# Layer 1's vertical convolution: odd taps from shared row sums, and the difference of sums on GpSimd

## The chip, the cores and the metric

The kernel runs on one core of one Trainium2 chip. The metric is device time in microseconds (us) of one execution. A profile of one execution was taken for each kernel; its engines are called PE (TensorE matmuls), PEld (TensorE weight loads), DVE (VectorE), ACT (ScalarE), POOL (GpSimd) and SP (SyncE, which issues the DMAs).

## What is computed

The input `x` has shape (2, 128, 256, 256), in float32. There are two residual layers. Layer 0 is group norm followed by windowed attention; the change does not touch it. Layer 1 is group norm followed by a convolution block, cut here to what matters:

```python
x = x + _L0_conv_ref(_gn(x), ...)            # attention
x = x + _L1_conv_ref(_gn(x), w1, w3, w4)

def _L1_conv_ref(x, w1, w3, w4):
    t1 = conv(x, w1, padding=((2, 2), (0, 0)))       # 128 -> 128 channels, 5 taps down the rows
    t3 = conv(t1, w3, padding=((1, 1), (0, 0)), feature_group_count=c)   # 3 taps, per channel
    t2 = _unfold_w3_dil2(x)                          # columns -2, 0, +2
    t4 = einsum('nckhw,ckg->nghw', t2, w4)           # 8 group maps
    return t4[:, None] * t3.reshape(n, c // g, g, h, w)
```

The heavy part is `t1`: each output row is the sum of five 128 x 128 products with five neighbouring input rows.

## The kernel before

The 128 channels lie on the 128 partitions. Layer 1 (`convolutions_fast`) runs over 64 strips of 8 rows, 32 for each of the two batch items. Each engine carries out its instructions in the order in which the program text issues them. Engines meet only at semaphores.

Strip `k` of the main loop issues this, in this order:

1. `load_rows1(k+2)`: DMAs from SP.
2. `unfold(k)` (line 645): twelve small matmuls for `t4`, which ACT copies out (line 651).
3. `first_rows(k)`: ACT copies the two top rows of `t1` and one row of `p1` from the strip before (lines 682 and 683). In the first strip of a batch item matmuls make them.
4. `start_strip(k+1)`: ACT copies four normalised rows (604) and DVE normalises eight new ones (606). At a batch start the group norm's coefficients come first (lines 117 to 140).
5. `vertical(k, 2)`: the first four rows of `t1`, then ACT scales them by the first tap of `w3` (line 711).
6. `row_sums(k+1)`: ACT copies two old sums (631), DVE adds neighbouring rows into four new ones (632).
7. `depthwise(k, 2)`: two DVE instructions with two SBUF inputs each add the other two taps of `w3` (718).
8. `vertical(k, 4)` for the other four rows; `spread(k)` (729): four matmuls that copy `t4` to 128 channels.
9. `combine` (738) of two quarters on DVE, `depthwise(k, 4)` (718), `combine` of the other two.
10. `finish(k)`: POOL adds the residual rows in two instructions (746: three rows; 747: five rows), SP stores the strip.

The vertical taps use a fast algorithm that makes two output rows with three products of two-tap or three-tap polyphase filters. In `vertical(k, m)`, p1 (odd taps on odd rows), p0 (even taps on even rows) and p2 (sums of taps on sums of rows) are one PSUM tile of 512 columns each, that is two rows for a pair of pairs. p1 takes 2 matmuls, p0 takes 3, p2 takes 3; so 8 matmuls of 512 columns for four rows. ACT copies p1 to SBUF (696). DVE makes the even row as p0 + delayed p1 (698), `both` as p0 + p1 (700) and the odd row as p2 - `both` (706). The PSUM tiles of `taps` come from a pool of three buffers, so the fourth tile waits until the first has been read.

Float32 matmuls stand in the profile as two records each.

Of the kernel before, what the change touches and what calls it, by code (L numbers as in the profile page):

```python
# [9 lines left out]
F32 = mybir.dt.float32  # L10
I32 = mybir.dt.int32
AF = mybir.ActivationFunctionType
ALU = mybir.AluOpType
# [6 lines left out]
P = 128  # L20
W = 256
# [530 lines left out]
def convolutions_fast(tc, io, x1_d, norm, st_y, out):  # L552

    nc = tc.nc
    NB, _, H, _ = io["x"].shape
    NS = H // 8
    with ExitStack() as l1:
        cst = l1.enter_context(tc.tile_pool(name="f_l1c", bufs=1))
        rawp = l1.enter_context(tc.tile_pool(name="f_raw1", bufs=6))
        tp = l1.enter_context(tc.tile_pool(name="f_t1", bufs=2))  # L560
        wk = l1.enter_context(tc.tile_pool(name="f_wk1", bufs=2))
        ps_pj = l1.enter_context(tc.tile_pool(name="f_ps_pj1", bufs=1, space=PSUM))
        ps_a = l1.enter_context(tc.tile_pool(name="f_ps_a", bufs=3, space=PSUM))
        ps_b = l1.enter_context(tc.tile_pool(name="f_ps_b", bufs=1, space=PSUM))

        w1 = cst.tile([P, 5, P], F32, tag="w1", name="w1")
# [5 lines left out]
        sel = cst.tile([P, P], F32, tag="sel", name="sel")  # L572
        nc.sync.dma_start(sel, io["c_sel"])

        w1s = cst.tile([P, 2, P], F32, tag="w1s", name="w1s")
        nc.vector.tensor_add(w1s[:, 0], w1[:, 4], w1[:, 3])
        nc.vector.tensor_add(w1s[:, 1], w1[:, 2], w1[:, 1])
        xn = [cst.tile([P, 12, 260], F32, tag=f"xm{i}", name=f"xm{i}") for i in range(2)]
        for i in range(2):
            nc.gpsimd.memset(xn[i], 0.0)  # L580
# [29 lines left out]
                nc.gpsimd.memset(cur[:, 4 + n : 12, :], 0.0)  # L610

        norms = {}
        t1s, sms, p1s = {}, {}, {}

# [8 lines left out]
        def row_sums(k):  # L625
            s = k % NS
            xt = xn[k % 2]
            sms[k] = sm = tp.tile([P, 6, W], F32, tag="sm", name=f"sm_{k}")
            lo = 0 if s == 0 else 2
            if s > 0:  # L630
                nc.scalar.copy(sm[:, 0:2], sms[k - 1][:, 4:6])
            nc.vector.tensor_tensor(
                sm[:, lo:6], xt[:, 2 * lo : 12 : 2, 2 : 2 + W], xt[:, 2 * lo + 1 : 12 : 2, 2 : 2 + W],
                ALU.add,
            )

        ts = {}

# [17 lines left out]
        def taps(name, n, terms):  # L656
            pa = ps_a.tile([P, 512], F32, tag="a", name=f"a_{name}")
            for i, (w, rows) in enumerate(terms):
                nc.tensor.matmul(pa[:, : n * W], w, rows, start=i == 0, stop=i == len(terms) - 1)  # L659
            return pa[:, : n * W].rearrange("p (r w) -> p r w", w=W)  # L660

        def first_rows(k):

            s = k % NS
            xt = xn[k % 2]

            t1s[k] = t1 = tp.tile([P, 10, W], F32, tag="t1", name=f"t1_{k}")
            p1s[k] = p1 = tp.tile([P, 5, W], F32, tag="p1", name=f"p1_{k}")
            if s == 0:
                nc.gpsimd.memset(t1[:, 0:1, :], 0.0)  # L670
                top = taps(
                    f"{k}_first", 1,
                    [(w1[:, tap], xt[:, tap - 1 : tap, 2 : 2 + W]) for tap in (2, 3, 4)],
                )
                nc.scalar.copy(t1[:, 1:2, :], top)
                top = taps(
                    f"{k}_p1", 1,
                    [(w1[:, 3 - 2 * i], xt[:, 3 - 2 * i : 4 - 2 * i, 2 : 2 + W]) for i in range(2)],
                )
                nc.scalar.copy(p1[:, 0:1], top)  # L680
            else:
                nc.scalar.copy(t1[:, 0:2, :], t1s[k - 1][:, 8:10, :])
                nc.scalar.copy(p1[:, 0:1], p1s[k - 1][:, 4:5])
            if s + 1 == NS:
                nc.gpsimd.memset(t1[:, 9:10, :], 0.0)

        def vertical(k, m):

            s = k % NS
            xt, sm, t1, p1 = xn[k % 2], sms[k], t1s[k], p1s[k]  # L690

            def rows(j):
                return xt[:, j : j + 3 : 2, 2 : 2 + W]

            pa = taps(f"{k}_p1_{m}", 2, [(w1[:, 3 - 2 * i], rows(2 * m + 1 - 2 * i)) for i in range(2)])
            nc.scalar.copy(p1[:, m - 1 : m + 1], pa)
            pa = taps(f"{k}_p0_{m}", 2, [(w1[:, 4 - 2 * i], rows(2 * m - 2 * i)) for i in range(3)])
            nc.vector.tensor_tensor(t1[:, 2 * m - 2 : 2 * m + 1 : 2, :], pa, p1[:, m - 2 : m], ALU.add)
            both = wk.tile([P, 2, W], F32, tag="both", name=f"both_{k}_{m}")
            nc.vector.tensor_tensor(both, pa, p1[:, m - 1 : m + 1], ALU.add)  # L700
            pa = taps(
                f"{k}_p2_{m}", 2,
                [(w, sm[:, m - i : m - i + 2]) for i, w in enumerate((w1s[:, 0], w1s[:, 1], w1[:, 0]))],
            )
            n = 1 if m == 4 and s + 1 == NS else 2
            nc.vector.tensor_tensor(  # L706
                t1[:, 2 * m - 1 : 2 * m + 2 * n - 2 : 2, :], pa[:, 0:n], both[:, 0:n], ALU.subtract
            )
            t3 = ts[k][1]
            j = 2 * m - 4  # L710
            nc.scalar.activation(t3[:, j : j + 4], t1[:, j : j + 4, :], AF.Copy, scale=w3[:, 0:1])  # L711
# [39 lines left out]
        with tc.manual_schedule(engines=ORDERED):  # L751
            for k in range(2):
                load_rows1(*divmod(k, NS))
            start_strip(0)
            row_sums(0)
            for k in range(NB * NS):
                more = k + 1 < NB * NS
                if k + 2 < NB * NS:
                    load_rows1(*divmod(k + 2, NS))
                unfold(k)  # L760
                first_rows(k)
                if more:
                    start_strip(k + 1)

                vertical(k, 2)
                if more:
                    row_sums(k + 1)
                depthwise(k, 2)
                vertical(k, 4)
                banks = spread(k)  # L770
                combine(k, banks, (0, 1))
                depthwise(k, 4)
                combine(k, banks, (2, 3))
                finish(k)


def kernel_body(tc, io, out):
    nc = tc.nc
    NB, _, H, _ = io["x"].shape
    NS = H // 8  # L780
    with ExitStack() as ctx:
        glob = ctx.enter_context(tc.tile_pool(name="f_glob", bufs=1))
        dram = ctx.enter_context(tc.tile_pool(name="f_dram", bufs=1, space=DRAM))
        small = ctx.enter_context(tc.tile_pool(name="f_small", bufs=4))
        gavg = glob.tile([P, P], F32, tag="f_gavg", name="f_gavg")
        nc.sync.dma_start(gavg, io["c_gavg"])
        x1_d = [
            [dram.tile([P, 8, W], F32, tag=f"f_x1_{b}_{s}", name=f"f_x1_{b}_{s}") for s in range(NS)]
            for b in range(NB)
        ]  # L790
        norm = Norms(nc, glob, small, gavg, NS)
        tags = ("f_st0", "f_st1", "f_st2")
        st_x, st_y = {0: norm.new("f_st_x0", tags[0])}, {}
        ends = glob.tile([P, NB * NS], F32, tag="f_ends", name="f_ends")
        attention_fast(tc, io, x1_d, norm, st_x, st_y, tags, ends)
        good = in_range(tc, glob, ends)
        convolutions_fast(tc, io, x1_d, norm, st_y, out)
        count = nc.values_load(good, min_val=0, max_val=P)
    with tc.If(count < P):
        tile_halo_attention_then_conv(tc, io, out)  # L800
# [567 lines left out]
```

## Time and profile before

| | |
|---|---|
| median of 3 runs | 3296.84 us (3296.19 to 3297.35) |
| the profiled execution's own time | 3296.72 us |
| its span, first to last instruction | 3294.9 us |
| layer 1 | about 2118 us to the end, 64 strips |
| one strip in the steady state | 17.73 us, between equal instructions of neighbouring strips |

In the timeline of PE one strip is the sum of three stretches: `spread` 2780.28 to 2781.35, `unfold` to 2784.07, and the vertical taps to 2798.01, when the next `spread` starts. In each of the two batch items 31 strips follow one another at this pace; at the change of batch PE is idle for 7.60 us on DVE's statistics (line 117).

How to read the rows: in a timeline row the columns are start in us, length in us, engine, line, operation, output and inputs, shape, count, and in brackets the engine's idle time before it with what ended it. Lengths of consecutive DVE instructions overlap a little, because one starts before the one ahead of it has fully retired; so sums of work use distances from start to start.

### The profile page before, as it was taken

Reading aid. Unit: us, or ns where it says so; the run is one execution under the profiler, and the core shown is the slowest. Engines: PE = TensorE matmul, PEld = TensorE weight load, DVE = VectorE, ACT = ScalarE, POOL = GpSimd, SP = SyncE. Lnnn points to the kernel's source line nnn. Section 1 sums busy time; section 2 is a strip of 40 time slices with the busy share of each in tenths; the row PEclk is TensorE's granted clock in tenths of the full one; section 3 lists DMA queues with packets and bytes.
Section 4 is the critical chain, followed back from the end, with each engine's and each line's share of the span. In section 5 each row is a group of like instructions: output and inputs, shape, how many; then the busy total and the mean of one; then the engine's idle time right before and its main releaser. Section 6 shows DMA issues by size and latency. Waiting matters only on the chain.

```text
span 3294.9 us, 117110 instructions
## 1 busy us (share of the span) xinstructions
PE 3143.8 (95%) x52798; PEld 2244.1 (68%) x52798; DVE 2628.0 (80%) x4083; ACT 1499.9 (46%) x2543; POOL 935.7 (28%) x978
## 2 busy tenths in 40 slices
PE   0799999999999999999999999899999989999997
PEld 0688998998998889889988898633333333333333
DVE  8678888888888777777777777588888888888887
ACT  0455555555555555555555555333333323333332
POOL 2222222222222122222222222133433333433433
PEclk9999999999999999999999999999999999999999
DMA  9333323323323122122222222233333333333332
GB/s 400 117 105 128 118 96 127 116 97 127 115 100 122 62 86 86 67 83 85 72 83 81 76 83 70 76 103 125 105 128 119 111 102 128 110 120 128 104 126 86
DMA packets 115899, 360.34 MB, mean 109 GB/s; under 512 B 8000, under 2 KB 74304, under 8 KB 90816
## 3 DMA queue, kind: packets, MB, share of 16 engines
q1 hardware_dynamic: 115392, 352.76, 30.2%
q8 instruction: 419, 6.86, 0.8%
q14 instruction: 88, 0.72, 0.1%
HBM read 218.51 MB, written 134.22 MB: 107 GB/s over the span
## 4 chain that ended last, share of the span: by engine, by line
PE 95%; issue 2%; DVE 1%; POOL 1%; DMA 1%; ACT 0%; SPq 0%; POOLq 0%; DVEq 0%
PE a_p L659 27%; PE f_pv L399 14%; PE f_pq L324 8%; PE f_s L434 8%; PE f_o L459 8%; PE f_pk L324 7%; PE f_py L324 7%; PE g L645 5%; PE f_pa L378 4%; PE f_s L418 4%; PE b L729 2%; DMA f_sx<-in_x 0%; DVE t L718 0%; POOL f_xn L189 0%; DMA raw<-f_x 0%
## 5 line engine op out<-in xcount | busy, mean ns | idle before, releaser
L405 DVE COPY f_vt<-f_pv 64x512 f32<-64x512 f32 x512 | 354.5, 695 | 299.2 <-ACT f_vt L405 299.0
L659 PE MATMUL a_p<-xm,w 128*128 128x512 f32 (+1 forms) x1288 | 580.5, 596 | 0.0
L306 POOL COPY f_xq<-f_xn 128x256 f32<-128x256 f32 x512 | 309.1, 648 | 763.7 <-DVE f_xn L292 763.7
L399 PE MATMUL f_pv<-f_wqkvT,f_xn 128*128 128x128 f32 x4096 | 491.3, 278 | 0.0
L399 PEld LDWEIGHTS f_pv<-f_wqkvT,f_xn 128*128 128x128 f32 x4096 | 466.9, 192 | 8.6
L659 PEld LDWEIGHTS a_p<-xm,w 128*128 128x128 f32 x1288 | 237.9, 188 | 330.8 <-issue 330.5
L443 ACT ACTIVATE f_p<-f_s 128x512 f32<-128x512 f32 x512 | 264.4, 604 | 406.0 <-PE f_s L434 406.0
L359 ACT ACTIVATE f_q<-f_pq,f_head 128x512 f32<-128x512 f32 x512 | 310.4, 688 | 297.1 <-PE f_pq L324 297.0
L711 ACT ACTIVATE t<-t,w 128x1024 f32<-128x1024 f32 x128 | 147.3, 1150 | 619.1 <-DVE t L706 619.1
L718 DVE SCALAR_TENSOR_TENSOR t<-t,w,t 128x1024 f32<-128x1024 f32 x256 | 420.2, 1642 | 6.8 <-ACT t L711 1.7
L405 ACT COPY f_vt<-f_pv 64x512 f32<-64x512 f32 x512 | 298.0, 582 | 119.0 <-PE f_pv L399 118.2
L746 POOL TENSOR_TENSOR y<-y,raw 128x768 f32<-128x768 f32 x62 | 169.5, 2734 | 540.1 <-DVE y L738 493.0
L283 POOL COPY f_xn<-f_xn 128x1280 f32<-128x1280 f32 x62 | 86.7, 1398 | 780.7 <-PE f_pv L399 780.7
L747 POOL TENSOR_TENSOR y<-y,raw 128x1280 f32<-128x1280 f32 x64 | 246.4, 3850 | 164.3 <-DVE y L738 164.3
L434 PEld LDWEIGHTS f_s<-f_q,f_kt 64*64 64x64 f32 x16384 | 251.6, 135 | 49.6 <-issue 49.2
L324 PE MATMUL f_pq<-f_xn,f_wq_s 128*128 128x160 f32 (+1 forms) x1536 | 277.0, 327 | 0.9 <-issue 0.9
L434 PE MATMUL f_s<-f_q,f_kt 64*64 64x64 f32 x16384 | 269.2, 220 | 0.0
L459 PE MATMUL f_o<-f_vt,f_p 128*32 128x66 f32 x16384 | 264.6, 223 | 0.0
L459 PEld LDWEIGHTS f_o<-f_vt,f_p 128*32 128x32 f32 x16384 | 243.2, 111 | 9.1
L324 PE MATMUL f_py<-f_ot,f_woT 128*128 128x256 f32 x1024 | 243.2, 380 | 2.3 <-DVE f_ot L477 2.3
L324 PE MATMUL f_pk<-f_xn,f_wqkvT 128*128 128x256 f32 x1024 | 245.3, 380 | 0.0
L324 PEld LDWEIGHTS f_pq<-f_xn,f_wq_s 128*128 128x128 f32 x1536 | 234.7, 188 | 13.9 <-issue 1.5
(117 smaller groups left out, 4377.4 us busy)
## 6 DMA issues: line engine op xcount, KB each, us to landing
f_raw<-in_x SPq DMA_DIRECT2D x62, 1280.0 KB, 8.2
f_sx<-in_x SPq DMA_DIRECT2D x64, 1024.0 KB, 7.6
f_x<-f_x SPq DMA_DIRECT2D x128, 512.0 KB, 3.4
out<-y SPq DMA_DIRECT2D x64, 1024.0 KB, 4.9
raw<-f_x SPq DMA_DIRECT2D x64, 640.0 KB, 6.4
raw<-f_x SPq DMA_DIRECT2D x62, 384.0 KB, 6.8
f_raw<-in_x SPq DMA_DIRECT2D x2, 1024.0 KB, 7.9
raw_pre<-f_x SPq DMA_DIRECT2D x2, 384.0 KB, 5.3
```

Source lines behind the costliest of these rows:

```text
L306: nc.gpsimd.tensor_copy(xq[:, t2, half].rearrange("p t r n c e -> p r t (n c) e"), cells[:, :, 16 * half : 16 * half + 16, 1 + t2 : 9 : 4, ...
L324: nc.tensor.matmul(dst[:, 32 * lo : 32 * hi], w, moving[:, lo:hi], start=True, stop=True)
L359: nc.scalar.activation(q[:, c, :, i], pq.rearrange("p (n x) -> p n x", n=NPAIR), AF.Copy, scale=head[:, i : i + 1],)
L399: nc.tensor.matmul(pv[:, P * n : P * n + P], xn[k % 2][:, r, 4 * j + n].rearrange("p c x -> p (c x)"), wvT, start=True, stop=True,)
L405: (nc.vector.tensor_copy if c else nc.scalar.copy)(vt[rows, 4 * j : 4 * j + 4, :, c, 0:32], pv[rows].rearrange("p (n h d) -> p n h d", n=4 ...
L434: nc.tensor.matmul(sc[g][n // 8][64 * c : 64 * c + 64, n % 8].rearrange("p i x -> p (i x)"), keys_k[rows, c, 48 * n : 48 * n + 64], qs[u][ ...
L443: nc.scalar.activation(pts[u][:, g, 8 * half : 8 * half + 8].rearrange("p n i x -> p (n i x)"), sc[g][half].rearrange("p n i x -> p (n i x ...
L459: nc.tensor.matmul(po[32 * h : 32 * h + 32, n - lo], p[:, h // 2, n, h % 2], vt[:, n, h], start=True, stop=True,)
L659: nc.tensor.matmul(pa[:, : n * W], w, rows, start=i == 0, stop=i == len(terms) - 1)
L718: nc.vector.scalar_tensor_tensor(t3[:, j : j + 4], t1[:, j + tap : j + tap + 4, :], w3[:, tap : tap + 1], t3[:, j : j + 4], ALU.mult, ALU.add,
L746: nc.gpsimd.tensor_tensor(y[:, 0:3, :], y[:, 0:3, :], raws[b, s - 1][:, 5:8, :], ALU.add)
L747: nc.gpsimd.tensor_tensor(y[:, 3:8, :], y[:, 3:8, :], raws[b, s][:, 0:5, :], ALU.add)
```

## The change

The five taps are split in another way. With the sum of rows 2i+1 and 2i+2 as `sm`, both rows of a pair share one term, the sum of taps 1 and 3 on `sm` (`both`), and one of two difference terms: tap 1 on the difference of neighbouring sums, or minus tap 3 on the next such difference (the tile `c` holds `both` plus these). The even row adds three taps on even-phase rows and the odd row three taps on odd-phase rows, with differences of weights. For four output rows this makes one matmul of 256 columns (c), two of 256 columns (d), three of 512 (e) and three of 512 (o).

Differences of sums, `df`, are made once per strip on POOL from `sm`. `sm` has five rows instead of six, of which ACT copies one from the strip before, and DVE still computes four. `p1` and its copies go. Six weight combinations are made at the start instead of two. On DVE the three instructions per `vertical` become `c` (from PSUM and a broadcast of `both`), the even row and the odd row, each with one PSUM and one SBUF input.

```diff
-        w1s = cst.tile([P, 2, P], F32, tag="w1s", name="w1s")
-        nc.vector.tensor_add(w1s[:, 0], w1[:, 4], w1[:, 3])
-        nc.vector.tensor_add(w1s[:, 1], w1[:, 2], w1[:, 1])
+        w1s = cst.tile([P, 6, P], F32, tag="w1s", name="w1s")
+        nc.vector.tensor_add(w1s[:, 0], w1[:, 1], w1[:, 3])
+        nc.vector.tensor_scalar(w1s[:, 1], w1[:, 3], -1.0, None, ALU.mult)
+        for i, (a, b) in enumerate(((2, 1), (4, 3), (0, 1), (2, 3))):
+            nc.vector.tensor_sub(w1s[:, 2 + i], w1[:, a], w1[:, b])
...
-            sms[k] = sm = tp.tile([P, 6, W], F32, tag="sm", name=f"sm_{k}")
-            lo = 0 if s == 0 else 2
+            sms[k] = sm = tp.tile([P, 5, W], F32, tag="sm", name=f"sm_{k}")
+            dfs[k] = df = tp.tile([P, 4, W], F32, tag="df", name=f"df_{k}")
+            lo = 0 if s == 0 else 1
             if s > 0:
-                nc.scalar.copy(sm[:, 0:2], sms[k - 1][:, 4:6])
+                nc.scalar.copy(sm[:, 0:1], sms[k - 1][:, 4:5])
             nc.vector.tensor_tensor(
-                sm[:, lo:6], xt[:, 2 * lo : 12 : 2, 2 : 2 + W], xt[:, 2 * lo + 1 : 12 : 2, 2 : 2 + W],
+                sm[:, lo:5], xt[:, 2 * lo + 1 : 10 : 2, 2 : 2 + W], xt[:, 2 * lo + 2 : 11 : 2, 2 : 2 + W],
                 ALU.add,
             )
+            nc.gpsimd.tensor_tensor(df, sm[:, 0:4], sm[:, 1:5], ALU.subtract)
...
-                top = taps(
-                    f"{k}_p1", 1,
-                    [(w1[:, 3 - 2 * i], xt[:, 3 - 2 * i : 4 - 2 * i, 2 : 2 + W]) for i in range(2)],
-                )
-                nc.scalar.copy(p1[:, 0:1], top)
             else:
                 nc.scalar.copy(t1[:, 0:2, :], t1s[k - 1][:, 8:10, :])
-                nc.scalar.copy(p1[:, 0:1], p1s[k - 1][:, 4:5])
...
-            pa = taps(f"{k}_p1_{m}", 2, [(w1[:, 3 - 2 * i], rows(2 * m + 1 - 2 * i)) for i in range(2)])
-            nc.scalar.copy(p1[:, m - 1 : m + 1], pa)
-            pa = taps(f"{k}_p0_{m}", 2, [(w1[:, 4 - 2 * i], rows(2 * m - 2 * i)) for i in range(3)])
-            nc.vector.tensor_tensor(t1[:, 2 * m - 2 : 2 * m + 1 : 2, :], pa, p1[:, m - 2 : m], ALU.add)
-            both = wk.tile([P, 2, W], F32, tag="both", name=f"both_{k}_{m}")
-            nc.vector.tensor_tensor(both, pa, p1[:, m - 1 : m + 1], ALU.add)
+            pa = taps(f"{k}_c_{m}", 1, [(w1s[:, 0], sm[:, m - 1 : m])])
+            both = wk.tile([P, 1, W], F32, tag="both", name=f"both_{k}_{m}")
+            nc.scalar.copy(both, pa)
+            pa = ps_a.tile([P, 512], F32, tag="a", name=f"a_{k}_d_{m}")
+            for i, w in enumerate((w1[:, 1], w1s[:, 1])):
+                nc.tensor.matmul(
+                    pa[:, W * i : W * i + W], w, df[:, m - 2 + i : m - 1 + i], start=True, stop=True
+                )
+            c = wk.tile([P, 2, W], F32, tag="c", name=f"c_{k}_{m}")
+            nc.vector.tensor_tensor(
+                c, pa.rearrange("p (r w) -> p r w", w=W), both.to_broadcast([P, 2, W]), ALU.add
+            )
             pa = taps(
-                f"{k}_p2_{m}", 2,
-                [(w, sm[:, m - i : m - i + 2]) for i, w in enumerate((w1s[:, 0], w1s[:, 1], w1[:, 0]))],
+                f"{k}_e_{m}", 2,
+                [(w, rows(2 * m - 4 + 2 * i)) for i, w in enumerate((w1[:, 0], w1s[:, 2], w1s[:, 3]))],
+            )
+            nc.vector.tensor_tensor(t1[:, 2 * m - 2 : 2 * m + 1 : 2, :], pa, c, ALU.add)
+            pa = taps(
+                f"{k}_o_{m}", 2,
+                [(w, rows(2 * m - 3 + 2 * i)) for i, w in enumerate((w1s[:, 4], w1s[:, 5], w1[:, 4]))],
             )
             n = 1 if m == 4 and s + 1 == NS else 2
             nc.vector.tensor_tensor(
-                t1[:, 2 * m - 1 : 2 * m + 2 * n - 2 : 2, :], pa[:, 0:n], both[:, 0:n], ALU.subtract
+                t1[:, 2 * m - 1 : 2 * m + 2 * n - 2 : 2, :], pa[:, 0:n], c[:, 0:n], ALU.add
             )
```

In the order of issue, `df` of strip k+1 stands on POOL ahead of the two instructions of `finish(k)`. The matmul pair d of a strip waits for it. The lines of the changed kernel used below are 608 (normalise), 638 (row sums), 642 (`df`), 704 (`c`), 711 (even rows), 717 (odd rows), 722 (ACT's scaling), 729 (`depthwise`), 749 (`combine`), 757 and 758 (`finish`).

More of the change, by code (lines that the diff above doesn't have):

```diff
@@ L612, in convolutions_fast @@
         norms = {}
-        t1s, sms, p1s = {}, {}, {}
+        t1s, sms, dfs = {}, {}, {}
         def start_strip(k):
@@ L667, in first_rows @@
             t1s[k] = t1 = tp.tile([P, 10, W], F32, tag="t1", name=f"t1_{k}")
-            p1s[k] = p1 = tp.tile([P, 5, W], F32, tag="p1", name=f"p1_{k}")
             if s == 0:
@@ L689, in vertical @@
             s = k % NS
-            xt, sm, t1, p1 = xn[k % 2], sms[k], t1s[k], p1s[k]
+            xt, sm, df, t1 = xn[k % 2], sms[k], dfs[k], t1s[k]
             def rows(j):
                 return xt[:, j : j + 3 : 2, 2 : 2 + W]
-            pa = taps(f"{k}_p1_{m}", 2, [(w1[:, 3 - 2 * i], rows(2 * m + 1 - 2 * i)) for i in range(2)])
-            nc.scalar.copy(p1[:, m - 1 : m + 1], pa)
-            pa = taps(f"{k}_p0_{m}", 2, [(w1[:, 4 - 2 * i], rows(2 * m - 2 * i)) for i in range(3)])
-            nc.vector.tensor_tensor(t1[:, 2 * m - 2 : 2 * m + 1 : 2, :], pa, p1[:, m - 2 : m], ALU.add)
-            both = wk.tile([P, 2, W], F32, tag="both", name=f"both_{k}_{m}")
-            nc.vector.tensor_tensor(both, pa, p1[:, m - 1 : m + 1], ALU.add)
-            pa = taps(
-                f"{k}_p2_{m}", 2,
-                [(w, sm[:, m - i : m - i + 2]) for i, w in enumerate((w1s[:, 0], w1s[:, 1], w1[:, 0]))],
+            pa = taps(f"{k}_c_{m}", 1, [(w1s[:, 0], sm[:, m - 1 : m])])
[10 more added lines that the diff above has]
+            )
+            pa = taps(
+                f"{k}_e_{m}", 2,
[5 more added lines that the diff above has]
+                [(w, rows(2 * m - 3 + 2 * i)) for i, w in enumerate((w1s[:, 4], w1s[:, 5], w1[:, 4]))],
             )
```

## The prediction

> **What bounds the kernel now.** I read the page's busy table first, then the chain that ended last, then the timeline of one strip for DVE and POOL.
>
> The page's first lines and its chain:
>
> ```profile
> span 3294.9 us, 117110 instructions
> PE 3143.8 (95%) x52798; PEld 2244.1 (68%) x52798; DVE 2628.0 (80%) x4083; ACT 1499.9 (46%) x2543; POOL 935.7 (28%) x978
> PE 95%; issue 2%; DVE 1%; POOL 1%; DMA 1%; ACT 0%; SPq 0%; POOLq 0%; DVEq 0%
> ```
>
> PE sets the end, so fewer matmul columns would count in full. But 80% for DVE is a mean over two layers. The busy table of a stretch inside layer 1 (columns: stretch, its length, busy us and instructions of each engine, clock, DMA) says more:
>
> ```profile
> 2150.00:2680.90 530.90, 530.90 (x1916) 207.76 (x1916) 460.52 (x480) 184.34 (x270) 198.60 (x62) 1.00 0.35 119
> ```
>
> Here PE is busy throughout and DVE for 460.52 of 530.90 us, 87%. A strip is 17.73 us, so DVE has 15.4 us of work in it and POOL 6.6. DVE is second, and closely.
>
> DVE through one strip (timeline of DVE):
>
> ```profile
> 2780.38 0.69 DVE L706 TENSOR_TENSOR t<-a_p,both 128x512 f32<-128x512 f32 x1 [1.10 <-PE a_p L659]
> 2781.49 1.29 DVE L738 TENSOR_TENSOR y<-b,t 128x512 f32<-128x512 f32 x2 [0.42 <-PE b L729]
> 2782.70 4.03 DVE L718 SCALAR_TENSOR_TENSOR t<-t,w,t 128x1024 f32<-128x1024 f32 x2
> 2786.83 1.29 DVE L738 TENSOR_TENSOR y<-b,t 128x512 f32<-128x512 f32 x2
> 2788.04 1.34 DVE L606 TENSOR_SCALAR xm<-raw,mean_y,rstd_y 128x2048 f32<-128x2048 f32 x1
> 2789.30 0.68 DVE L698 TENSOR_TENSOR t<-a_p,p 128x512 f32<-128x512 f32 x1
> 2789.90 0.68 DVE L700 TENSOR_TENSOR both<-a_p,p 128x512 f32<-128x512 f32 x1
> 2791.25 0.69 DVE L706 TENSOR_TENSOR t<-a_p,both 128x512 f32<-128x512 f32 x1 [0.67 <-PE a_p L659]
> 2791.86 1.36 DVE L632 TENSOR_TENSOR sm<-xm 128x1024 f32<-128x1024 f32 x1
> 2793.21 2.61 DVE L718 SCALAR_TENSOR_TENSOR t<-t,w,t 128x1024 f32<-128x1024 f32 x2
> 2795.74 0.68 DVE L698 TENSOR_TENSOR t<-a_p,p 128x512 f32<-128x512 f32 x1
> ```
>
> POOL over the same time, and the ranges (min/median/max in ns) of two lines from the views by source line:
>
> ```profile
> 2782.91 2.73 POOL L746 TENSOR_TENSOR y<-y,raw 128x768 f32<-128x768 f32 x1 [8.51 <-DVE y L738]
> 2788.20 3.93 POOL L747 TENSOR_TENSOR y<-y,raw 128x1280 f32<-128x1280 f32 x1 [2.56 <-DVE y L738]
> ...
> L718 DVE SCALAR_TENSOR_TENSOR t<-t,w,t x256: 1273/1285/2729, 2141.6 to 3280.5; 128x1024 f32<-128x1024 f32 x128
> ...
> L747 POOL TENSOR_TENSOR y<-y,raw x64: 2876/3930/3940, 2154.2 to 3284.6; 128x1280 f32<-128x1280 f32 x64
> ```
>
> Only 2.2 us of the strip are DVE waits on PE (1.10, 0.42, 0.67). And two equal L718 pairs take 2.61 and 4.03 us: the long one lies beside POOL's L746. One L718 is 1.285 us or 2.73 us, not something between. L747 is 2.88 us alone (the last one) and 3.93 beside L606.
>
> **What the Trainium skill says.** "SBUF — State Buffer", section "Who interferes with whom": a DVE instruction with two SBUF inputs and a GpSimd instruction that reads SBUF exclude each other; whichever starts first keeps the shared port for its whole length and the other blocks. A DVE instruction with one SBUF input, outside the two-port modes, does not contend. The trace agrees: L746 waits out the first L718 (to 2783.98), runs to 2785.64, and the second L718 ends 1.09 us later; L698, with one PSUM input, stays at 0.68 beside L747. "Perfetto Trace Analysis", section "GPSIMD Engine Instruction", warns not to trust a POOL span; so I price POOL by what DVE loses. "TensorE: Matmul & The Clock Gate", section "What's actually happening": an idle window of some 3.4 us halves PE's clock; here ten records took 6.21 us after the idle of 7.60 us at the batch change, 4.46 otherwise.
>
> **PE.** Removed per strip: 16 matmuls of 512 columns. Added: 12 of 512 and 6 of 256. A record of 512 columns is 0.43 us (its weight loads stand 0.43 apart), a matmul two, 0.86. Eight records of 256 in attention take 1.75 us from start to start (1399.74 to 1401.49), 0.22 each, so the weight load of 0.19 still hides. PE per strip: 17.73 - 16 x 0.86 + 12 x 0.86 + 6 x 0.44 = 16.9 us. If PE stayed the bound, that is 0.8 us x 64 = 53 us less.
>
> **ACT and setup.** ACT does less: L696's 0.58 us copy halves, the sums' copy (0.60) halves, L683 (0.41) goes; at 46% load it stays off the path. Its copy of `both` is queued behind its L722, which waits for L717, but is done at about 5.2 in the layout below and wanted at 9.7. Four more weight combinations at 0.29 us lie in DVE's 0.97 us wait for a DMA before the first strip, to within 0.2 us. No DMA changes.
>
> **DVE's own work.** Three instructions per `vertical` stay three, one PSUM and one SBUF input each: 0.60 us start to start. One thing is new: L711 reads the `c` that L704 just wrote, so it must wait until L704 has retired. Two dependent L718 stand 1.32 apart, 0.03 over one's length; so 0.72 instead of 0.60, +0.12, twice per strip. Before, L698 and L700 were independent.
>
> **POOL's `df` (L642).** 1024 elements, both inputs in SBUF. It becomes ready about 0.13 us after the row sums L638 end (the delay from DVE's end to L746 at 2782.91), while DVE's first L729 starts at once. So it will wait out that L729 and hold off the second, as L746 does now. No row has 1024 elements. From below: L746's 768 elements cost DVE 4.03 - 2.60 = 1.43 us. Slope: L746 ran 1.66 us after L718 let go, L747 2.75 us after L606 did (2789.38 to 2792.13), so 1.09 us for 512 elements. That gives 1.43 + 0.55 = 1.98 us; from above, 1280 elements, 2.52. I take 1.98. Behind `df` on POOL stands L757, which needs it gone by 13.0 below; the matmul d that waits for `df` (e and o behind it) comes at 12.9; `df` is done at 8.7. So only the port costs.
>
> **DVE's strip laid out**, from the start of L608 at 0:
> - L608, then L704 at 1.26, L711 at 1.98, L717 at 2.58. PE is not awaited here if DVE is the later one.
> - L638 wants the port at 3.19. L758 took it when L608 ended and keeps it to 4.09. L632 ended 1.09 us after L747; so L638 ends at 5.18, as before (2793.22 - 2788.04). The 0.67 us wait on PE that goes here becomes a wait on POOL.
> - L729 twice with `df` in between: 5.17 + 2.53 + 1.98 = 9.68, when L704 starts. Then L711 10.40, L717 11.00.
> - L749 twice. ACT's scaling ended 1.88 us after L706's start (2782.26) and L729 can follow 0.03 later: 12.91.
> - The rest, 2782.70 to 2788.04, is unchanged: 5.34. Sum 18.25 us.
>
> PE's deadlines in this: o ends about 8.7 (awaited at 11.0), `spread` 9.8 (11.6), the next d 13.8 and o 19.0 (19.5 and 20.8). So DVE waits on PE nowhere, and PE now waits some 1.4 us a strip for PSUM tiles that DVE has yet to read. A strip costs 18.25 instead of 17.73, +0.52.
>
> **The sum.** The first strip's PE work is 1.1 us shorter, and its DVE strip not yet blocked by an L758: -1.2. 29 strips at +0.52: +15.1. Towards the batch change, where the five-row normalise spares the L638 block: +0.8. At the change PE is restarted by DVE, and its next two strips are the shorter ones: -2.3. 30 more: +15.6, +0.2. The last strip has no `df` and runs at PE's pace: -1.6. Together +26.6, on the profiled 3296.72: 3323.3. That execution lies 0.1 us under the median 3296.84; so 3323.
>
> **Rivals.**
> - *PE stays the bound (faster).* `df` would have to slip into the 3.2 us from 9.7 to 12.9 where DVE works from PSUM, or its block be short. DVE without it is 16.3 us plus what it then waits; under about 0.6 us of block PE's 16.9 decides, and the time is 3297 - 53 - 1 = 3243. Up to 1.46 us of block (17.73 - 16.27) it is still faster than before. Against: the smaller L746 already costs 1.43 in the same position. For: the arbitration between two dependent L718 is seen only there.
> - *No change.* A block at the lower end, 1.43 us, makes a strip of 17.70; with the ends' -4 us, about 3291 to 3300.
> - *Slower still.* `df` at 2.52 gives 18.79 a strip, +1.06 x 60 - 4 = +60: 3357. Or PE's new pauses of 1.4 us drop its clock; the page's window of 3.4 us speaks against it, as do the 16.9 us of work between.
>
> **How the numbers follow.** Forecast (DVE bound, 3306 to 3340) 0.63; no change 0.12; PE bound or between, down to 3240, 0.14; slower still 0.11. The range leaves most of the two outer cases out: 3278 to 3350. What a measurement can tell from no change is about 0.2%, 6.6 us. Faster than that: 0.14 and a third of the no-change case, 0.18; same 0.09; slower 0.73.
>
> **What would show it.** Right: strips 18.2 us apart; in DVE's timeline both L729 pairs long, the first near 4.6 us; DVE's waits on PE gone; PE idle by 1 to 1.5 us a strip on DVE's L704 and L711; POOL busier by some 3 us a strip. Wrong: a first L729 pair of 2.6 us, or PE without idle at 16.9 a strip (PE bound); L704 to L711 0.60 apart (no self-wait); L638 undisturbed at 1.22 us.

## The result, and the profile after

| | before | changed |
|---|---|---|
| median of 4 runs | 3296.69 us | 3324.34 us (3322.96 to 3324.87) |
| ratio to before | 1 | 1.0082 (95% interval 1.0069 to 1.0095) |
| profiled execution, its span | 3296.72, 3294.9 us | 3322.96, 3321.2 us |

The kernel became slower by 0.8%. The page's busy table and its chain:

```profile
span 3321.2 us, 117667 instructions
PE 3119.7 (94%) x53046; PEld 2281.4 (69%) x53046; DVE 2779.1 (84%) x4087; ACT 1438.4 (43%) x2479; POOL 1149.5 (35%) x1042
PE 63%; DVE 25%; issue 10%; POOL 1%; DMA 1%; ACT 0%; DVEq 0%; SPq 0%; POOLq 0%
```

PE's busy time fell by 24 us, yet the span grew by 26. The chain says why: PE led 95% of it before, 63% now; a quarter runs over DVE and a tenth is "issue", time in which the engine waited for nothing that the profile shows. The busy table of the same stretch inside layer 1:

```profile
2150.00:2680.90 530.90, 507.23 (x1978) 219.32 (x1977) 518.39 (x465) 151.44 (x234) 291.63 (x88) 1.00 0.34 114
```

PE is now idle for 4.5% of the stretch (0.8 us of each strip), DVE for 2.4%. POOL went from 37% to 55%. DVE waited 2.2 us a strip for PE before; now its table of waits over nearly the same time (to 2680; the columns are the total in us, how often, and the longest) is down to two single events:

```profile
DVE t L711 <- DVE c L704: 0.5, 1, 0.5
DVE y L749 <- PE a_e L666: 0.5, 1, 0.5
```

One strip in DVE's timeline, with POOL's below it:

```profile
2802.90 1.34 DVE L608 TENSOR_SCALAR xm<-raw,mean_y,rstd_y 128x2048 f32<-128x2048 f32 x1
2804.16 0.68 DVE L704 TENSOR_TENSOR c<-a_d,both 128x512 f32<-128x512 f32 x1
2804.95 0.69 DVE L711 TENSOR_TENSOR t<-a_e,c 128x512 f32<-128x512 f32 x1
2805.55 0.68 DVE L717 TENSOR_TENSOR t<-a_o,c 128x512 f32<-128x512 f32 x1
2806.15 1.94 DVE L638 TENSOR_TENSOR sm<-xm 128x1024 f32<-128x1024 f32 x1
2808.01 4.56 DVE L729 SCALAR_TENSOR_TENSOR t<-t,w,t 128x1024 f32<-128x1024 f32 x2
2812.50 0.68 DVE L704 TENSOR_TENSOR c<-a_d,both 128x512 f32<-128x512 f32 x1
2813.28 0.69 DVE L711 TENSOR_TENSOR t<-a_e,c 128x512 f32<-128x512 f32 x1
2813.89 0.68 DVE L717 TENSOR_TENSOR t<-a_o,c 128x512 f32<-128x512 f32 x1
2814.49 1.28 DVE L749 TENSOR_TENSOR y<-b,t 128x512 f32<-128x512 f32 x2
2815.79 4.04 DVE L729 SCALAR_TENSOR_TENSOR t<-t,w,t 128x1024 f32<-128x1024 f32 x2
2819.93 1.29 DVE L749 TENSOR_TENSOR y<-b,t 128x512 f32<-128x512 f32 x2
2821.14 1.34 DVE L608 TENSOR_SCALAR xm<-raw,mean_y,rstd_y 128x2048 f32<-128x2048 f32 x1
```

```profile
2803.07 3.94 POOL L758 TENSOR_TENSOR y<-y,raw 128x1280 f32<-128x1280 f32 x1 [2.56 <-DVE y L749]
2808.26 3.24 POOL L642 TENSOR_TENSOR df<-sm 128x1024 f32<-128x1024 f32 x1 [1.25 <-DVE sm L638]
2815.89 2.85 POOL L757 TENSOR_TENSOR y<-y,raw 128x768 f32<-128x768 f32 x1 [4.40 <-DVE y L749]
```

From one L608 to the next it is 18.24 us. No row of DVE has an idle time in brackets. The first L729 pair, which took 2.61 us before, takes 4.56, with `df` (L642) beside it. The row sums L638 take 1.94 us and end 1.08 us after L758 does. These waits stand inside the lengths of instructions, so they count as busy: DVE's 97.6% holds some 4.1 us a strip by which instructions are longer than alone: 1.95 in the first pair, 1.43 in the second (as before, beside L757), 0.72 in L638 (1.22 alone; 0.14 before). The timeline names no releaser for them. The description of the kernel before says that engines meet only at semaphores; DVE and POOL meet here without one, at the port, and the table of waits has no row for that.

PE waits where DVE has not yet read a PSUM tile (PE's timeline):

```profile
2803.18 1.02 PE L666 MATMUL a_o<-xm,w 128*128 128x512 f32 x2
2804.89 0.70 PE L666 MATMUL a_c<-sm,w1s 128*128 128x256 f32 x2 [0.70 <-DVE c L704]
2805.69 0.70 PE L700 MATMUL a_d<-df,w 128*128 128x256 f32 x2
```

The c of the second half needs the tile that the first half's d occupied, and L704 frees it; the d behind it needs the tile of the first half's e, which L711 frees.

### The profile page after: what moved, and what is told of

Read it like the earlier page. It is cut to its first block, busy times and chain, and to the rows that moved or that the text cites. A ratio compares the mean times of both kernels' runs of the same rounds, so it can differ in the third digit from the quotient of the medians.

```text
span 3321.2 us, 117667 instructions
## 1 busy us (share of the span) xinstructions
PE 3119.7 (94%) x53046; PEld 2281.4 (69%) x53046; DVE 2779.1 (84%) x4087; ACT 1438.4 (43%) x2479; POOL 1149.5 (35%) x1042
## 4 chain that ended last, share of the span: by engine, by line
PE 63%; DVE 25%; issue 10%; POOL 1%; DMA 1%; ACT 0%; DVEq 0%; SPq 0%; POOLq 0%
PE f_pv L399 14%; DVE t L729 9%; PE f_pq L324 8%; PE f_s L434 8%; PE f_o L459 8%; PE f_pk L324 7%; PE f_py L324 7%; PE f_pa L378 4%; PE f_s L418 4%; DVE y L749 4%; DVE sm L638 3%; DVE c L704 2%; DVE xm L608 2%; DVE t L717 2%; DVE t L711 1%
## 5 line engine op out<-in xcount | busy, mean ns | idle before, releaser
L729 DVE SCALAR_TENSOR_TENSOR t<-t,w,t 128x1024 f32<-128x1024 f32 x256 | 544.0, 2125 | 8.0 <-ACT t L722 1.9
L758 POOL TENSOR_TENSOR y<-y,raw 128x1280 f32<-128x1280 f32 x64 | 246.4, 3851 | 163.9 <-DVE y L749 163.9
L757 POOL TENSOR_TENSOR y<-y,raw 128x768 f32<-128x768 f32 x62 | 176.4, 2845 | 275.8 <-DVE y L749 268.4
L642 POOL TENSOR_TENSOR df<-sm 128x1024 f32<-128x1024 f32 x64 | 206.8, 3232 | 105.1 <-DVE sm L638 89.4
L666 PE MATMUL a_e<-xm,w1s 128*128 128x512 f32 x512 | 240.7, 591 | 0.0
```

Source lines behind the costliest of these rows:

```text
L642: nc.gpsimd.tensor_tensor(df, sm[:, 0:4], sm[:, 1:5], ALU.subtract)
L729: nc.vector.scalar_tensor_tensor(t3[:, j : j + 4], t1[:, j + tap : j + tap + 4, :], w3[:, tap : tap + 1], t3[:, j : j + 4], ALU.mult, ALU.add,
L758: nc.gpsimd.tensor_tensor(y[:, 3:8, :], y[:, 3:8, :], raws[b, s][:, 0:5, :], ALU.add)
```

## The experiments

The port theory: DVE bounds the changed kernel, because `df` keeps the shared port from the second L729. Its rivals: the new matmul shapes and tile waits slow PE (PE theory); PE waits for POOL's result, or POOL's being busy is what costs (latency theory); another order of issue gains by itself, without the change. Ratios are to the kernel before, timed again beside each group of runs; its medians lie between 3296.69 and 3298.83 us, so times of different groups compare to about 2 us.

**Without `df`.**

```diff
+        zero = cst.tile([P, 4, W], F32, tag="zero", name="zero")
+        nc.gpsimd.memset(zero, 0.0)
...
-            dfs[k] = df = tp.tile([P, 4, W], F32, tag="df", name=f"df_{k}")
+            dfs[k] = zero
...
-            nc.gpsimd.tensor_tensor(df, sm[:, 0:4], sm[:, 1:5], ALU.subtract)
```

> The changed kernel without the subtraction on POOL: the differences of the row sums are left out, the matmuls d read a tile of zeros that is written once. Port theory (DVE bounds the changed kernel, and df costs it 1.96 us a strip by holding the shared port between the two L729): DVE falls to 18.24 - 1.96 = 16.28 us a strip, PE's 16.9 bounds, time 3243 to 3252, first L729 pair 2.6 us. Rival PE theory (narrower matmuls, more weight loads and waits for PSUM tiles make PE slower): nothing changes on PE, 3315 or more.

3244.61 us, ratio 0.9833 (0.9817 to 0.9850). The busy table of 2150 to 2660 and DVE's timeline (the two added lines shift the numbers: L730 is `depthwise`):

```profile
2150.00:2660.00 510.00, 507.65 (x2046) 230.35 (x2040) 479.15 (x482) 157.10 (x242) 201.71 (x62) 1.00 0.37 124
...
2412.98 2.59 DVE L730 SCALAR_TENSOR_TENSOR t<-t,w,t 128x1024 f32<-128x1024 f32 x2
```

The first pair is back at 2.59 us. PE is busy for 507.65 of 510 us (487.14 in the changed kernel), at 16.88 us a strip (from the first `combine` row, 2401.33, to the next, 2418.21). So the new matmuls are worth what their columns say, and nothing on PE made the change slow: the PE theory falls. This run also takes POOL's result away, so it leaves the latency theory open.

**POOL writes, but does not read.**

```diff
-            dfs[k] = df = tp.tile([P, 4, W], F32, tag="df", name=f"df_{k}")
+            dfs[k] = df = tp.tile([P, 10, W], F32, tag="df", name=f"df_{k}")
...
-            nc.gpsimd.tensor_tensor(df, sm[:, 0:4], sm[:, 1:5], ALU.subtract)
+            nc.gpsimd.memset(df, 0.0)
```

> In place of the subtraction POOL writes zeros (memset of 2560 elements, about 2.2 us at the 2.67 us that 3120 elements took before the first strip), at the same place and with the same readers; the differences are left out of the result. Port theory: a POOL instruction that only writes doesn't keep out DVE instructions with two SBUF inputs, so as without df: 3243 to 3252, first L729 pair 2.6 us. Rival latency theory (what costs is that PE waits for POOL, or POOL's own occupancy): as the changed kernel, 3315 to 3325.

3245.10 us, ratio 0.9834 (0.9817 to 0.9850). DVE's and POOL's timelines:

```profile
2412.91 1.80 DVE L638 TENSOR_TENSOR sm<-xm 128x1024 f32<-128x1024 f32 x1
2414.62 2.59 DVE L729 SCALAR_TENSOR_TENSOR t<-t,w,t 128x1024 f32<-128x1024 f32 x2
...
2409.68 3.94 POOL L758 TENSOR_TENSOR y<-y,raw 128x1280 f32<-128x1280 f32 x1 [2.55 <-PE a_e L666]
2413.56 2.23 POOL L642 MEMSET df<- 128x2560 f32 x1
```

The memset runs from 2413.56 to 2415.79; its 2.23 us are close to the 2.38 that `df` takes alone (the reordered kernel below). POOL is busy for 267 of 510 us in this kernel and for 280 in the changed one. Beside the memset run L638 (2412.91 to 2414.71, freed by L758 at 2413.62) and most of the first L729, both with two SBUF inputs, and neither is late: L638 ends 1.09 us after L758 as always, the pair takes 2.59 us. So it is POOL's reading that keeps these DVE instructions out, not POOL being busy, as the Trainium skill's "SBUF — State Buffer" has it in "Who interferes with whom". The memset waits for no row sums and starts earlier than `df` did, so PE has its tile sooner; that PE's wait for POOL is not what costs is shown by the run with an unread `df` below.

**The subtraction on DVE.**

```diff
-            nc.gpsimd.tensor_tensor(df, sm[:, 0:4], sm[:, 1:5], ALU.subtract)
+            nc.vector.tensor_tensor(df, sm[:, 0:4], sm[:, 1:5], ALU.subtract)
```

> The same subtraction on DVE, right behind the row sums. Port theory: DVE pays about 1.2 us itself and 0.1 for reading the row sums just written, but no longer 1.96 of blocking: 18.24 - 1.96 + 1.26 = 17.54 us a strip, about 3282. Rival: if DVE's load alone were what counts, adding an instruction to the busiest engine makes it slower than 3324.

3285.81 us, ratio 0.9963 (0.9949 to 0.9977); 17.59 us a strip (L608 at 2400.55 and 2418.14).

```profile
2405.84 1.23 DVE L642 TENSOR_TENSOR df<-sm 128x1024 f32<-128x1024 f32 x1
2406.98 2.60 DVE L729 SCALAR_TENSOR_TENSOR t<-t,w,t 128x1024 f32<-128x1024 f32 x2
```

Giving the work back to the engine that bounds is some 39 us faster than taking it off: 1.23 us of its own, and about 0.1 of waiting for the row sums just written, instead of 1.95 us of blocking.

**The kernel before, with `df` added and read by nobody.**

```diff
+            df = tp.tile([P, 4, W], F32, tag="df", name=f"df_{k}")
+            nc.gpsimd.tensor_tensor(df, sm[:, 0:4], sm[:, 1:5], ALU.subtract)
```

> The kernel before with one instruction more: POOL subtracts neighbouring row sums (1024 elements) behind the row sums of each strip, into a tile that nothing reads. Port theory: first L718 pair 4.56 us, DVE becomes the bound at about 18.12 us a strip, 3297 + 0.39 x 60 - 2 = 3318. Rivals (PE theory, latency theory): nothing waits for it, 3297.

3327.90 us, ratio 1.0089 (1.0072 to 1.0106). That is the whole slowdown, without the change's matmuls and with no reader to wait for POOL: the latency theory falls. The expectation was 10 us low: a strip takes 18.24 us, not 18.12. Its DVE timeline (here the new lines shift the numbers: L702 makes `both`, L708 the odd row, L720 is `depthwise`):

```profile
2416.01 4.56 DVE L720 SCALAR_TENSOR_TENSOR t<-t,w,t 128x1024 f32<-128x1024 f32 x2
2420.49 0.68 DVE L700 TENSOR_TENSOR t<-a_p,p 128x512 f32<-128x512 f32 x1
2421.09 0.68 DVE L702 TENSOR_TENSOR both<-a_p,p 128x512 f32<-128x512 f32 x1
2421.88 0.69 DVE L708 TENSOR_TENSOR t<-a_p,both 128x512 f32<-128x512 f32 x1
```

L702 to L708 is 0.79 us where L700 to L702 is 0.60: the odd row reads the `both` just written. The kernel before has the same pair of instructions; there the odd row waits longer, for PE (1.35 us from `both` in the strip shown in the prediction), which hides this.

**The even rows add an older `c`.**

```diff
+        old = {}
...
+            prev = old.get(0, c)
+            old[0] = c
...
-            nc.vector.tensor_tensor(t1[:, 2 * m - 2 : 2 * m + 1 : 2, :], pa, c, ALU.add)
+            nc.vector.tensor_tensor(t1[:, 2 * m - 2 : 2 * m + 1 : 2, :], pa, prev, ALU.add)
```

> The changed kernel with the even rows (L711) adding the c of the vertical before, instead of the one that L704 has just written; the even rows are computed from the wrong c, all instructions stay. Self-wait theory: L704 to L711 is 0.60 us instead of 0.79. In the first half of the strip the row sums' end is set by L758, so only the second vertical counts: 0.19 x 60 = 11 us less, about 3313. If both counted: 3302. If the self-wait cost nothing: 3324.

3312.37 us, ratio to before 1.0043 (1.0026 to 1.0059), 12 us less than the changed kernel. The rows of the second half (L705 makes `c` here, L714 the even rows):

```profile
2415.25 0.68 DVE L705 TENSOR_TENSOR c<-a_d,both 128x512 f32<-128x512 f32 x1
2415.85 0.68 DVE L714 TENSOR_TENSOR t<-a_e,c 128x512 f32<-128x512 f32 x1
```

From `c` to the even rows it is 0.60 us in both halves. In the first half the row sums only wait longer instead (2.13 us for 1.94), so half of the saving is lost there, as was expected.

**Another order of issue.**

```diff
+                vertical(k, 2)
                 if more:
                     start_strip(k + 1)
-
-                vertical(k, 2)
+                depthwise(k, 2)
                 if more:
                     row_sums(k + 1)
-                depthwise(k, 2)
```

> The changed kernel in another order of issue: the next strip's normalise after vertical 2, the row sums and df after the two L729 instead of ahead of them. df then lies beside L704, L711, L717 and L749, which read PSUM. Port theory: both costs go (first L729 pair 2.6 us, row sums 1.2 us), DVE comes to about 16.5 us and PE's 16.9 bounds: 3245 to 3260, faster than before. Rival PE theory: no faster than 3297. Rival: if order of issue matters little, 3315 to 3325.

3239.42 us, ratio 0.9820 (0.9804 to 0.9837). It leaves nothing out and beats both kernels: 1.8% under before, some 2.6% under the changed kernel (3239.42 / 3324.34 = 0.974). The busy table of 2150 to 2660 and the timelines of DVE and POOL:

```profile
2150.00:2660.00 510.00, 510.00 (x2051) 231.86 (x2050) 463.47 (x483) 157.24 (x243) 245.10 (x92) 1.00 0.37 124
...
2409.73 0.69 DVE L717 TENSOR_TENSOR t<-a_o,c 128x512 f32<-128x512 f32 x1 [1.13 <-PE a_o L666]
2411.70 2.60 DVE L729 SCALAR_TENSOR_TENSOR t<-t,w,t 128x1024 f32<-128x1024 f32 x2
2414.22 1.22 DVE L638 TENSOR_TENSOR sm<-xm 128x1024 f32<-128x1024 f32 x1
2417.35 1.28 DVE L749 TENSOR_TENSOR y<-b,t 128x512 f32<-128x512 f32 x2
...
2415.61 2.38 POOL L642 TENSOR_TENSOR df<-sm 128x1024 f32<-128x1024 f32 x1 [5.43 <-DVE sm L638]
```

`df` now runs from 2415.61 to 2417.99, beside instructions that read PSUM, and it holds nothing off. L638 is back at 1.22 us, DVE waits for PE again, and PE is busy all the time. The second L729 pair still takes 4.04 us beside L757; with PE as the bound that costs nothing.

Each half of this order alone, and the order on the kernel before:

> One half of e4: the normalise stays where the change has it, only the row sums and df go behind the two L729. Port theory: df lies beside PSUM work and blocks nothing; DVE waits some 1.2 us for ACT's scaling where the row sums stood, but is clear of L758 by then. DVE comes to about 16.9 us a strip, level with PE: 3243 to 3262. If both halves were needed: near 3297.

> The other half of e4: only the normalise moves behind vertical 2; row sums and df stay ahead of the two L729. Port theory: L758 now holds off the normalise instead of the row sums, and df still lies between the two L729 (pair 4.56 us): about 18.2 us a strip, 3315 to 3328. If the normalise's place were what e4 gained from: 3245 to 3260.

> The kernel before with the order of issue of e4 (normalise after vertical 2, row sums after the two L718). PE bounds it at 17.73 us a strip either way: 3297, within 3. If the order alone were what gains, about 1% less.

| only this moved | time, us | ratio to before |
|---|---|---|
| row sums and `df` behind the two L729 | 3247.24 | 0.9847 (0.9831 to 0.9863) |
| normalise behind `vertical(k, 2)` | 3348.39 | 1.0156 (1.0139 to 1.0173) |
| both, in the kernel before | 3294.83 | 0.9989 (0.9982 to 0.9996) |

The place of the row sums and of `df` behind them is what counts. With only these moved, the first L729 pair and `df` read:

```profile
2414.77 2.60 DVE L729 SCALAR_TENSOR_TENSOR t<-t,w,t 128x1024 f32<-128x1024 f32 x2 [1.28 <-ACT t L722]
...
2418.68 2.38 POOL L642 TENSOR_TENSOR df<-sm 128x1024 f32<-128x1024 f32 x1 [4.42 <-DVE sm L638]
```

The order by itself gains 0.1% in the kernel before. The normalise alone makes the changed kernel worse by 24 us, 20 above the upper end of what was expected. In its DVE and POOL timelines:

```profile
2401.04 2.16 DVE L608 TENSOR_SCALAR xm<-raw,mean_y,rstd_y 128x2048 f32<-128x2048 f32 x1
2403.41 1.22 DVE L638 TENSOR_TENSOR sm<-xm 128x1024 f32<-128x1024 f32 x1 [0.20 <-ACT xm L606]
2404.55 4.56 DVE L729 SCALAR_TENSOR_TENSOR t<-t,w,t 128x1024 f32<-128x1024 f32 x2
...
2399.22 2.91 POOL L758 TENSOR_TENSOR y<-y,raw 128x1280 f32<-128x1280 f32 x1 [2.55 <-DVE y L749]
```

L608 now waits for L758: it takes 2.16 us for 1.34 and ends 1.07 us after L758's end at 2402.13. L638 waits 0.20 us for ACT's copied rows, and `df` still falls between the L729. So two SBUF inputs are not the only case: L608 reads one large SBUF tensor, and it and L758 shut each other out as well. Which of the two is held up depends on which starts first: in the changed kernel L608 starts first, keeps its 1.34 us, and L758 takes 3.94 for 2.91. With the sums moved too, this place of the normalise pays a little (3239.42 against 3247.24 us).

## Why the prediction was right

It said 3323; the median is 3324.34. By its steps:

- **PE.** 16.9 us a strip if PE were the bound: the kernel without `df` has 16.88. The saving is written as 0.8 x 64 = 53 us, which is 51; 53 comes from 17.73 - 16.9 = 0.83. Measured without `df`: 3298.83 - 3244.61 = 54 us.
- **The price of `df`.** 1.98 us was forecast; the first pair grew from 2.61 to 4.56, so 1.95. The length on POOL's row (3.24 us) would have misled: alone it takes 2.38.
- **The strip.** Laid out as 18.25, measured 18.24 in the strip shown. L638 ended 5.19 us after L608's start (5.18 forecast), L717 of the second half started at 10.99 (11.00), L729 at 12.89 (12.91).
- **The wait on its own result.** 0.72 us from L704 to L711 was forecast from two dependent L718; it is 0.79. The text called it new, which was wrong: the kernel before has the same wait between `both` and the odd row. The sum does not show the 0.07 us that were missing: in the first half they disappear in the wait for L758, and in the second L704 came 0.08 us earlier than laid out (9.60 for 9.68), which is luck.
- **The sum and the ends.** Forecast +26.6 on the profiled execution, measured 3322.96 - 3296.72 = +26.2. The total is closer than its parts, and that much is luck. Over the 58 strips of the steady stretches the normalise starts 17.73 us apart before and 18.23 after, on average, so they add 29.0 us where 58 x 0.52 = 30.2 was forecast; the start, the batch change and the end take off 2.8 us where the forecast's terms leave 3.6.
- **PE's pauses.** 1 to 1.5 us a strip was forecast; the busy table shows 0.8. Between the starts of matmuls it is 0.85 us before c and 0.36 before d (at 2805.69), beyond the 0.43 and 0.22 us of each record ahead of them, 1.2 in all: the busy row covers part of a pause, because it counts a matmul to its modelled end. The granted clock in the stretch stays at 1.00, so the clock rival did not occur.
- **The faster rival.** It needed `df` to slip into the stretch where DVE works from PSUM. It does not do so on its own, but when the order is changed it does.

That `df` costs the port is true of the place that the change gives it. With two calls of the loop exchanged, `row_sums` behind `depthwise`, the same instruction holds nothing off.

## What to carry to other kernels

Before moving elementwise work to GpSimd, look at what VectorE does at that moment. In this kernel its additions with two SBUF inputs, and the normalise too, ran one after the other with a GpSimd instruction that reads SBUF, so the transfer can cost more than it saves. Issue such work where VectorE reads PSUM. And when the bound engine is relieved by 5%, check that the second one, here at 87%, has room for what the change makes it wait: waits for a port are counted as busy and do not show in a table of waits.

## What the runs showed that was not expected

The kernel before was within one unread POOL instruction of being bound by DVE: 1024 elements a strip made it 0.9% slower. And a DVE addition of 512 elements that reads what the one ahead of it wrote starts 0.79 us after it, where an independent one starts after 0.60. Of these 0.19 us, 0.11 are a gap (the one ahead is 0.68 us long) for which the timeline names no releaser, and 0.08 are the overlap that is missing.
